# One numbering of expert blocks over eight sequences, worked off in two stages: 71 blocks a layer in place of 55 + 23

## The chip, the cores and the metric

The kernel runs on one core of a Trainium2 chip. The metric is the time of one execution on the device in microseconds (us), as a median of several runs. Profiles are taken from one further execution each. Of the core's engines, TensorE (PE) multiplies matrices and transposes, VectorE (DVE) and ScalarE (ACT) do element-wise work, GpSimd (POOL) does some of that and issues the indirect DMAs, and SyncE (SP) issues most other DMAs. PEld is TensorE's weight load, which overlaps the matmuls.

## What is computed

Input x has 8 sequences of 512 tokens with 256 features, all in float32. Four layers follow one another, each added to x:

```
x = x + attention_a(layernorm(x))   # 16 heads of 64, causal, with ALiBi
x = x + moe(layernorm(x))           # "f1"
x = x + attention_b(layernorm(x))   # 8 heads of 128, causal, rotary
x = x + moe(layernorm(x))           # "f2", the same weights

def moe(x):                         # 8 experts, each token goes to 2 of them
    h = rms_norm(x) * norm_w
    vals, idx = top_k(h @ gate_w.T + gate_b, 2)
    w = softmax(vals)
    t = h @ mlp1_w[e].T + mlp1_b[e]           # 512 wide: glu and lin
    a = min(glu, 7) * sigmoid(1.702 * glu) * (clip(lin, -7, 7) + 1)
    y[e] = a @ mlp2_w[e].T + mlp2_b[e]        # 256 wide
    return x + sum over the two experts of w * y[e]
```

The change touches the two expert layers alone. There are 8 x 512 x 2 = 8,192 pairs of a token and an expert in each.

## The kernel before, in words

**Sorted blocks.** Class `Experts` (line 533) serves one expert layer. `choose` (L645) picks each token's two experts, `count` (L701) counts how many pairs each expert has so far (`run`) and so gives each pair a place within its expert (`at`). Every expert's pairs are rounded up to whole blocks of 128 rows; a block thus has one expert and one set of weights. How many blocks each expert needs depends on the data, so the program has as many blocks as the worst case needs. The sequences form two groups, `GROUPS` (0 to 5, and 6 and 7), each numbered on its own: (6,144 + 8 x 127) / 128 gives 55 blocks, (2,048 + 8 x 127) / 128 gives 23. That is 78 blocks a layer. Each group has its own DRAM tables: `h_all` (normed rows to gather from) and `y_all` (results by token, `PLANE` rows for a token's first expert, as many for the second, and spare rows for empty slots).

**Sorting a group** (`sorting`, L865) has one piece per sequence and one more. The first piece calls `slots` (L726), which rounds the counts up, adds the expert's start to every place and splits the slot into block and row; it also gives each block's expert, by a comparison of the block's start with the experts' ends, and from it the column offsets of weights and biases (`we_at`, `be_at`). `pair` (L789) makes one-hot matrices of rows (`row`) and blocks (`col`) for one sequence, `invert` (L825) multiplies them on TensorE and adds the result into `sum`, and `tokens` (L839) turns that into the numbers of the token to gather and of the row to write. All of it but the product runs on VectorE.

**One step a block.** `run` (L984) walks n over all blocks. Step n does: `gather` of block n+4 (L886, an indirect DMA on GpSimd; 128 rows of 1 KB), `turn_act` of block n-4 (two transposes `atp` L948, ScalarE copy `aT` L952), `turn_rows` of block n (two transposes `gtp` L899, ScalarE copy back into the gather tile `g` L902), `first` of block n-1 (four matmuls recorded for `hp` L923; VectorE adds the bias L934, ScalarE's sigmoid L935, VectorE L937 to L939 make the product `a`), `second` of block n-5 (four matmuls recorded for `y` L961, VectorE adds the bias L971, GpSimd writes the rows by an indirect DMA L972), and then whatever pieces of other work are noted for step n in `aside`. Gather tiles hold `ROWS` = 4 blocks, in two buffers, and a group starts a new tile; the tiles of results `y` do the same.

**What sets the order.** TensorE's order is the program's, written out by hand (`manual_schedule` for PE). On the other engines a scheduler orders the instructions, save those that `keep_in_program_order` binds (ScalarE's copies and sigmoid among them). Each engine works in its order. `aside` places the work around the blocks: the end of the attention before (`flush`, L1125), the sort of the second group in pieces at steps 17, 21 and 25, and the start of what follows. The sort of the first group lies in the last sequences of the attention (`layer`, L1066).

**Ends of the layers.** Results may be read once all of a group's blocks are written; `read` (L1011) has a wait on every write of the group. With `done` = 55 + 6 = 61, the end of the first expert layer places in its steps: reading the rows of sequence 0 (`collect`, L1026, at done and done+1), adding them (`add`, L1042, line L1051, one 128-token tile a step from done+3), layer norm (done+8, +9, +11) and the first projections of attention b (`project` at steps 77 and 78, `values` at 80 and 81). The sequences 1 to 7 are added during attention b. At the end of f2, twelve halves of the sequences 0 to 5 are read at done + 3k/2 and finished four steps later (`finish`, L1178: four L1051 operations and an output DMA on SP, L1180); the four halves of sequences 6 and 7 are read after the last block, on SP's and ACT's queues.

## Time and profile before

| | |
|---|---|
| time, median of 3 runs | 2318.38 us (2312.13 to 2318.58) |
| time of the profiled execution | 2280.75 us |
| its span, first to last instruction | 2279.0 us |
| mean granted clock of TensorE | 0.994 |
| blocks, both layers | 156 |
| first hp of f1, last hp of f1 | at 932.7, at 1178.1 us |
| first hp of f2, last hp of f2 | at 2005.6, at 2249.4 us |
| DMA, mean over the span | 49 GB/s |

Lines of the profile name the source line of kernel.py, the engine, the operation, out <- in by the program's names, the shapes and the count; after the first bar the busy time and the mean of one in ns, after the second the engine's idle time just before, and what ended it. In a timeline the first two columns are start and duration in us. In the table of windows each engine has its busy time and count, then follow the granted clock, DMA share and GB/s. A matmul's name appears once for a run of instructions that start together ("x4"), and its duration is then that of the run. Where the profile says L923, TensorE multiplies a block by its expert's first weights; where it says L934, VectorE adds the bias to that.

### The profile page before, as it was taken

To read this page: it belongs to the slowest core of one execution; us is meant where nothing else is said; L and a number is where in the kernel's file an instruction comes from. 1 tells how busy PE (TensorE), PEld (TensorE's weight loads), DVE (VectorE), ACT (ScalarE), POOL (GpSimd) and SP (SyncE) were. 2 spreads that over 40 slices of the span, in tenths; PEclk is the share of its full clock that TensorE was granted. 3 is DMA by queue.
4 is the path that set the end of the run, shared out by engine and by line. 5 is a ranking of instruction groups with operands and counts; after the bars stand their busy time and mean duration, and the time that the engine had idled before them with its cause. 6 is when DMAs were issued, how large, how long until landed. Compare 5 with 4: busy or idle time off the path is not lost.

```text
span 2279.0 us, 34315 instructions
## 1 busy us (share of the span) xinstructions
PE 2227.7 (98%) x10681; PEld 1454.4 (64%) x10681; DVE 1597.6 (70%) x4773; ACT 972.3 (43%) x2826; POOL 995.3 (44%) x1365
## 2 busy tenths in 40 slices
PE   8999999999999999999999999999999999999995
PEld 5666666666666666666665666666666666666663
DVE  4566666666666677687777677777767678868677
ACT  4555555555555554333324334343434333433331
POOL 5443434343434342466654343333434344356663
PEclk9999999999999999999999999999999999999998
DMA  7100000000000000422320010110101000132246
GB/s 243 38 22 7 20 10 20 10 20 10 20 10 19 14 5 30 145 83 88 107 65 15 10 38 13 35 34 18 42 5 42 10 28 1 52 116 88 85 150 207
DMA packets 79731, 112.53 MB, mean 49 GB/s; under 512 B 10016, under 2 KB 64448, under 8 KB 79552
## 3 DMA queue, kind: packets, MB, share of 16 engines
q1 hardware_dynamic: 62656, 67.58, 8.9%
q0 software_dynamic: 14976, 40.91, 5.9%
q8 instruction: 89, 1.46, 0.3%
q10 hardware_dynamic: 1920, 1.84, 0.2%
q14 instruction: 90, 0.74, 0.1%
HBM read 68.86 MB, written 41.44 MB: 48 GB/s over the span
## 4 chain that ended last, share of the span: by engine, by line
PE 88%; DVE 6%; DMA 2%; issue 1%; ACT 1%; POOL 1%; SPq 0%; DVEq 0%; POOLq 0%; ACTq 0%
PE hp_f L923 10%; PE pp_b L327 9%; PE pp_a L327 9%; PE op_a L466 6%; PE tp_a L439 6%; PE sp_a L385 6%; PE sp_b L385 6%; PE op_b L466 5%; PE yp_a L484 5%; PE yp_b L484 5%; PE y_f L961 5%; PE vp_a L308 4%; PE vp_b L308 4%; PE tp_b L439 3%; PE gtp_f L899 1%; PE atp_f L948 1%
## 5 line engine op out<-in xcount | busy, mean ns | idle before, releaser
L407 ACT ACTIVATE S_a<-S_a,nm_a 128x512 f32<-128x512 f32 (+3 forms) x512 | 280.3, 549 | 311.8 <-DVE nm_a L397 311.7
L340 POOL TENSOR_TENSOR qk_b<-qk_b,rot_b 128x512 f32<-128x512 f32 x128 | 163.0, 1274 | 457.9 <-DVE qk_b L339 449.7
L923 PE MATMUL hp_f<-we,g_f 128*128 x624 | 294.7, 595 | 3.9 <-ACT g_f L902 3.9
L366 POOL TENSOR_SCALAR ali_a<-alibi 128x512 f32<-128x512 f32 x128 | 79.6, 622 | 455.6 <-DVE nm_a L397 443.1
L407 ACT ACTIVATE S_b<-S_b,nm_b 128x512 f32<-128x512 f32 (+3 forms) x256 | 142.8, 558 | 239.7 <-DVE nm_b L397 237.2
L397 DVE CUSTOM_DVE_ANT_0 S_a<-sp_a,ali_a 128x512 f32<-128x512 f32 (+3 forms) x512 | 215.8, 487 | 30.5 <-PE sp_a L385 30.5
L424 POOL TENSOR_SCALAR S_a<-S_a,sum_a 128x384 f32<-128x384 f32 x378 | 202.6, 554 | 34.9 <-DVE sum_a L418 26.4
L972 POOL DMA_INDIRECT y_f<-y_f,row_f x156 | 158.2, 1014 | 112.9 <-DVE y_f L971 67.0
L935 ACT ACTIVATE u_f<-u_f 128x256 f32<-128x256 f32 x156 | 65.1, 417 | 318.6 <-DVE u_f L934 304.8
L886 POOL DMA_INDIRECT g_f<-h_all_f,token_f x156 | 156.7, 1005 | 71.9 <-issue 68.3
L397 DVE CUSTOM_DVE_ANT_0 S_b<-sp_b,mask 128x512 f32<-128x512 f32 (+3 forms) x256 | 119.1, 484 | 90.8 <-PE sp_b L385 90.8
L385 PE MATMUL sp_b<-qk_b 128*128 128x512 f32 (+3 forms) x512 | 171.8, 438 | 8.1 <-POOL qk_b L340 8.1
L439 PE MATMUL tp_a<-ident,S_a 128*128 128x128 f32 x1280 | 166.7, 277 | 4.3 <-DVE O_a L474 3.2
L961 PEld LDWEIGHTS y_f<-we,aT_f 128*128 128x128 f32 x624 | 118.0, 190 | 82.1 <-issue 46.4
L934 DVE TENSOR_TENSOR u_f<-hp_f,be 128x512 f32<-128x512 f32 x156 | 107.8, 691 | 82.2 <-PE hp_f L923 75.1
L439 PEld LDWEIGHTS tp_a<-ident,S_a 128*128 128x128 f32 x1280 | 141.6, 141 | 35.5 <-issue 21.3
L961 PE MATMUL y_f<-we,aT_f 128*128 x624 | 160.2, 379 | 2.6 <-ACT aT_f L952 2.6
L466 PE MATMUL op_a<-PT_a,V_a 128*64 128x384 f32 (+3 forms) x1024 | 154.5, 439 | 3.6 <-ACT PT_a L449 2.2
L923 PEld LDWEIGHTS hp_f<-we,g_f 128*128 128x128 f32 x624 | 106.3, 190 | 80.7 <-issue 74.6
L385 PE MATMUL sp_a<-qk_a 64*128 64x512 f32 (+3 forms) x1024 | 155.5, 443 | 0.9 <-DVE qk_a L344 0.9
L449 ACT COPY PT_a<-tp_a 128x512 f32<-128x512 f32 (+1 forms) x320 | 139.0, 497 | 27.1 <-PE tp_a L439 26.8
L466 PE MATMUL op_b<-PT_b,V_b 128*128 128x512 f32 (+3 forms) x512 | 148.6, 433 | 0.0
(185 smaller groups left out, 4460.1 us busy)
## 6 DMA issues: line engine op xcount, KB each, us to landing
h_all_f<-hn_f SPq DMA_DIRECT2D x64, 128.0 KB, 1.7
xm_f<-x_mid_f SPq DMA_DIRECT2D x16, 512.0 KB, 4.0
yg_f<-y_f SPq DMA_DIRECT2D x32, 256.0 KB, 4.2
yg_f<-y_f SPq DMA_DIRECT2D x56, 128.0 KB, 2.2
we<-w_dram SPq DMA_DIRECT2D x8, 512.0 KB, 7.3
x_mid_f<-x SPq DMA_DIRECT2D x8, 512.0 KB, 3.4
x_mid_f<-xm_f SPq DMA_DIRECT2D x8, 512.0 KB, 2.9
x<-x_in_dram SPq DMA_DIRECT2D x7, 512.0 KB, 4.1
```

The lines of the kernel that those rows point to most:

```text
L308: nc.tensor.matmul(vp[:, k, :], lhsT=self.xT[b][:, c, t * P : (t + 1) * P], rhs=wv[:, c, q * 2 * P : (q + 1) * 2 * P], start=(c == 0), sto ...
L327: nc.tensor.matmul(pp, lhsT=w[:, c, g * P : (g + 1) * P], rhs=self.xT[b][:, c, :], start=(c == 0), stop=(c == NC - 1),)
L340: nc.gpsimd.tensor_tensor(qk[:, j, :], qk[:, j, :], rot, ALU.add)
L385: nc.tensor.matmul(sp[i][:, at[it] : at[it] + w], lhsT=qk[r, 0, it * P : (it + 1) * P], rhs=qk[r, 1, 0:w], start=True, stop=True,)
L397: nc.vector.tensor_tensor_reduce(out=s, in0=sp[i][:, at[it] : at[it] + w], in1=add[i][:, T - w : T], scale=scale, scalar=float(np.finfo(np ...
L407: nc.scalar.activation(s, s, AF.Exp, bias=nm[:, it : it + 1], scale=-1.0, accum_out=sums[:, it : it + 1],)
L424: eng.tensor_scalar(s, s, sums[:, it : it + 1], 1.0, ALU.mult, ALU.mult)
L439: nc.tensor.transpose(tp[:, o : o + P], S[:, S_OFF[it] + jt * P : S_OFF[it] + (jt + 1) * P], ident,)
L466: nc.tensor.matmul(op[i * cols : (i + 1) * cols, jt * P : T], lhsT=v[:, jt, c0 : c0 + cols], rhs=PT[i][:, P_OFF[jt] : P_OFF[jt] + T - jt * P],
L484: nc.tensor.matmul(yp[:, 0:D], lhsT=o[:, c, t * P : (t + 1) * P], rhs=wo[:, half * HALF + c, :], start=(c == 0), stop=(c == HALF - 1),)
L923: nc.tensor.matmul(hp, lhsT=h[:, c * P : (c + 1) * P], rhs=we_sb[:, bass.DynSlice(wat + c * 2 * FI, 2 * FI)], start=(c == 0), stop=(c == N ...
L961: nc.tensor.matmul(yp, lhsT=aT[:, c * P : (c + 1) * P], rhs=we_sb[:, bass.DynSlice(wat + NC * 2 * FI + c * D, D)], start=(c == 0), stop=(c ...
```

## The change

The eight sequences now have one numbering of blocks a layer, (8,192 + 8 x 127) / 128 = 71, which is worked off in two stages. The numbers go first to the blocks that the first six sequences fill entirely (of each expert in turn), then to each expert's one begun block, then to blocks that only the last two sequences need. Of the first six sequences' 6,144 pairs at most 8 x 127 are in begun blocks, so at least 41 blocks (`FULL`) are always full: stage 0 is blocks 0 to 40, stage 1 is the 30 others, whose rows may come from all eight sequences. The pairs of the first six lie in the first 55 blocks (`TOUCHED`), so their one-hot matrices stay 55 wide; those of the last two are 30 wide (`REACH`). There is one `h_all` and one `y_all` a layer.

A new piece `sizes` rounds the counts down and up, keeps three sizes for each expert and the running ends and shifts over the 3 x 8 of them, and calls `experts`, which in stage 1 compares each block with 24 ends. `slots` makes three products and reductions for each of a token's two choices, where there was one. Stage 0's sort has one piece more, in the attention; stage 1's has four, at steps 16, 20, 24 and 28. `done` is 60. Reads of the first six sequences wait for the first 55 writes and are declared independent of the later ones. The end of f1 is closer together (add at 63 and 64, norm at 65, 66 and 68, `project` at 69 and 70, `values` at 73 and 74). The last step is 75; of f2's twelve halves eight are finished at steps 64 to 74, and four after the last step. Line numbers move: L886 becomes L936, L899 L949, L902 L952, L923 L973, L934 to L939 become L984 to L989, L948 and L952 become L998 and L1002, L961 L1011, L971 and L972 become L1021 and L1022, L1013 L1067, L1051 L1107, L1180 L1233.

The core of the diff; what is cut renames the tables, opens them once for all sequences and passes `sum` by slices.

```diff
-GROUPS = [(0, 6), (6, 8)]
-BLOCKS = [(2 * (hi - lo) * T + NE * (P - 1)) // P for lo, hi in GROUPS]
-NJ = max(BLOCKS)
-PLANE = 32 * P
+STAGES = [(0, 6), (6, NB)]
+PAIRS = 2 * STAGES[0][1] * T
+SPARE = NE * (P - 1)
+FULL = -((SPARE - PAIRS) // P)
+TOUCHED = (PAIRS + SPARE) // P
+TOTAL = (2 * NB * T + SPARE) // P
+BLOCKS = [FULL, TOTAL - FULL]
+FIRST = [0, FULL]
+REACH = [(0, TOUCHED), (FULL, TOTAL)]
+PLANE = NB * T
...
-            self.h_all = [
-                dram.tile([(hi - lo) * T, D], F32, tag=f"h_{kind}_{i}", name=f"h_all_{kind}_{i}")
-                for i, (lo, hi) in enumerate(GROUPS)
-            ]
-            self.y_all = [
-                dram.tile([2 * PLANE + n * P, D], F32, tag=f"y_{kind}_{i}", name=f"y_{kind}_{i}")
-                for i, n in enumerate(BLOCKS)
-            ]
-            self.group_of = {b: i for i, (lo, hi) in enumerate(GROUPS) for b in range(lo, hi)}
...
+        def blocks_up(self, i, out, counts, add):
+            whole = self.rt(i, [P, NE], "whole", I32)
+            nc.vector.tensor_scalar_add(whole, counts, float(add))
+            nc.vector.tensor_scalar(
+                whole, whole, 7, 7, ALU.logical_shift_right, ALU.logical_shift_left
+            )
+            nc.vector.tensor_copy(out, whole)
+        def sizes(self, i):
+            r = self.R
+            size, end, shift, up = r["size"], r["end"], r["shift"], r["up"]
+            limit = self.rt(i, [P, NE], "limit")
+            turn = self.rt(i, [P, NE], "turn")
+            if i == 0:
+                nc.vector.memset(r["sum"], 0.0)
+                nc.vector.memset(size[:, 2, :], 0.0)
+                self.blocks_up(i, size[:, 0, :], r["run"], 0)
+                self.blocks_up(i, up, r["run"], P - 1)
+                nc.vector.tensor_tensor(size[:, 1, :], up, size[:, 0, :], ALU.subtract)
+                nc.vector.tensor_copy(limit, size[:, 0, :])
+            else:
+                self.blocks_up(i, size[:, 2, :], r["run"], P - 1)
+                nc.vector.tensor_tensor(size[:, 2, :], size[:, 2, :], up, ALU.subtract)
+                nc.vector.tensor_copy(limit, up)
+            flat = [x.rearrange("p a e -> p (a e)") for x in (end, size, shift)]
+            nc.vector.tensor_tensor_scan(
+                flat[0], ones[:, 0 : 3 * NE], flat[1], 0.0, ALU.mult, ALU.add
+            )
+            nc.vector.tensor_tensor(flat[2], flat[0], flat[1], ALU.subtract)
+            nc.vector.tensor_tensor(shift[:, 1, :], shift[:, 1, :], size[:, 0, :], ALU.subtract)
+            nc.vector.tensor_tensor(shift[:, 2, :], shift[:, 2, :], up, ALU.subtract)
+            nc.vector.tensor_tensor(turn, shift[:, i + 1, :], shift[:, i, :], ALU.subtract)
+            self.moves = shift[:, i, :], limit, turn
+            self.experts(i)
+        def experts(self, i):
...
+            parts = 1 if i == 0 else 3
+            ends = r["end"].rearrange("p a e -> p (a e)")[:, 0 : parts * NE]
             expert = self.rt(i, [P, nj], "expert")
-            for j0 in range(0, nj, 32):
-                j1 = min(j0 + 32, nj)
-                wide = [P, j1 - j0, NE]
+            most = D // (parts * NE)
+            for j0 in range(0, nj, most):
+                j1 = min(j0 + most, nj)
+                wide = [P, j1 - j0, parts * NE]
                 past = work.tile(wide, F32, tag="kb", bufs=8, name=f"past_{kind}_{i}_{j0}")
                 nc.vector.tensor_tensor(
                     past,
-                    end.unsqueeze(1).to_broadcast(wide),
-                    step_p[:, j0:j1].unsqueeze(2).to_broadcast(wide),
+                    ends.unsqueeze(1).to_broadcast(wide),
+                    step_p[:, FIRST[i] + j0 : FIRST[i] + j1].unsqueeze(2).to_broadcast(wide),
...
+            if parts > 1:
+                number = self.rt(i, [P, nj], "number", I32)
+                nc.vector.tensor_copy(number, expert)
+                nc.vector.tensor_single_scalar(number, number, NE - 1, ALU.bitwise_and)
+                nc.vector.tensor_copy(expert, number)
...
+        def slots(self, i):
+            kind = self.kind
+            r = self.R
+            lo, hi = STAGES[i]
+            here = slice(lo * NT, hi * NT)
+            n = (hi - lo) * NT
+            for k in range(2):
+                own = work.tile([P, 3, n], F32, tag="kb", bufs=8, name=f"own_{kind}_{i}_{k}")
+                for m, move in enumerate(self.moves):
+                    o = work.tile([P, n, NE], F32, tag="kb", bufs=8, name=f"of_{kind}_{i}_{k}_{m}")
+                    nc.vector.tensor_tensor(
+                        o, r["pick"][k][:, here, :], move.unsqueeze(1).to_broadcast([P, n, NE]), ALU.mult
+                    )
+                    nc.vector.tensor_reduce(own[:, m, :], o, AX.X, ALU.add)
+                by, limit, turn = (own[:, m, :] for m in range(3))
+                at = r["at"][:, k, here]
+                nc.vector.tensor_tensor(limit, at, limit, ALU.is_ge)
+                nc.vector.tensor_tensor(turn, turn, limit, ALU.mult)
+                nc.vector.tensor_tensor(by, by, turn, ALU.add)
+                nc.vector.tensor_tensor(at, at, by, ALU.add)
+            number = work.tile([P, 2, 2, n], I32, tag="kb", bufs=8, name=f"number_{kind}_{i}")
+            low, high = number[:, 0], number[:, 1]
+            nc.vector.tensor_copy(high, r["at"][:, :, here])
+            nc.vector.tensor_single_scalar(low, high, P - 1, ALU.bitwise_and)
+            nc.vector.tensor_single_scalar(high, high, 7, ALU.logical_shift_right)
+            nc.vector.tensor_copy(r["low"][:, :, here], low)
+            nc.vector.tensor_copy(r["high"][:, :, here], high)
...
-            here = slice(s * NT, (s + 1) * NT)
+            r, here = self.place(s)
+            j0, j1 = REACH[i]
+            nj = j1 - j0
...
         def sorting(self, i):
-            n = GROUPS[i][1] - GROUPS[i][0]
+            lo, hi = STAGES[i]
             def piece(s):
-                if s == 0:
+                if s == lo:
                     self.slots(i)
-                if s < n:
+                if s < hi:
                     self.pair(i, s)
-                if s > 0:
+                if s > lo:
                     self.invert(i, s - 1)
-                if s == n:
+                if s == hi:
                     self.tokens(i)
-            return [lambda s=s: piece(s) for s in range(n + 1)]
+            return [lambda: self.sizes(i)] + [lambda s=s: piece(s) for s in range(lo, hi + 1)]
...
-                in_=self.h_all[i],
-                in_offset=bass.IndirectOffsetOnAxis(ap=self.R[i]["token"][:, j : j + 1], axis=0),
+                in_=self.h_all[0 : STAGES[i][1] * T, :],
+                in_offset=bass.IndirectOffsetOnAxis(ap=self.R["token"][i][:, j : j + 1], axis=0),
...
+            if len(self.writes) >= TOUCHED:
+                tc.declare_no_dep(
+                    made.ins, group=f"reads_{self.kind}", reason="no rows of the first stage"
+                )
+            self.writes.append(made.ins)
...
+            early = b < STAGES[0][1]
+            writes = self.writes[0 : TOUCHED if early else TOTAL]
+            for write in writes:
...
+            if early:
+                for write in self.writes[TOUCHED:]:
+                    tc.declare_no_dep(made.ins, write, reason="no rows of the first stage")
+                tc.add_to_no_dep_group(f"reads_{self.kind}", made.ins)
...
-        at = [(6, 7, 1), (7, 0, 1), (7, 1, 1), (7, 2, 1), (7, 3, 1), (7, 4, 1), (7, 6, 1)]
+        at = [(6, 7, 1), (6, 7, 2), (7, 0, 1), (7, 1, 1), (7, 2, 1), (7, 3, 1), (7, 4, 1), (7, 6, 1)]
...
-            aside[17 + 4 * n] = [piece]
+            aside[16 + 4 * n] = [piece]
...
-    done = BLOCKS[0] + 6
+    done = TOUCHED + 5
...
     aside[done] = [lambda: exp_a.fetch(0)]
     for k, tag in enumerate(("xT", "PT")):
         tt = (2 * k, 2 * k + 1)
-        aside.setdefault(done + k, []).append(
-            lambda tt=tt, tag=tag: exp_a.collect(0, tt, tag, both_queues)
-        )
-        for t in tt:
-            aside.setdefault(done + t + 3, []).append(lambda tt=tt, t=t: exp_a.add(0, tt, (t,)))
-    aside[done + 8] = [lambda: att_b.norm(0)]
-    aside[done + 9] = [lambda: att_b.apply(0)]
-    aside[done + 11] = [lambda: att_b.turn_norm(0)]
+        aside[done].append(lambda tt=tt, tag=tag: exp_a.collect(0, tt, tag, both_queues))
+        aside[done + 3 + k] = [lambda tt=tt: exp_a.add(0, tt)]
+    aside[done + 5] = [lambda: att_b.norm(0)]
+    aside[done + 6] = [lambda: att_b.apply(0)]
+    aside[done + 8] = [lambda: att_b.turn_norm(0)]
     for k in range(2):
-        aside[sum(BLOCKS) - 1 + k] = [lambda k=k: att_b.project(0, 0, k)]
-        aside[sum(BLOCKS) + 2 + k] = [lambda k=k: att_b.values(0, 0, k)]
+        aside[TOTAL - 2 + k] = [lambda k=k: att_b.project(0, 0, k)]
+        aside[TOTAL + 2 + k] = [lambda k=k: att_b.values(0, 0, k)]
     exp_a.run(aside)
...
-    end = sum(BLOCKS) + 5
+    end = TOTAL + 5
     exp_b.run(aside)
     for m in range(end, n + 5):
         for piece in aside.get(m, ()):
             piece()
-    last = [(b, tt) for b in range(*GROUPS[1]) for tt in ((0, 1), (2, 3))]
+    last = [(b, tt) for b in range(*STAGES[1]) for tt in ((0, 1), (2, 3))]
```

## The prediction

> **What bounds the kernel now.** I read the page first: engine shares, the chain that ended last, then the expert rows.
>
> ```profile
> PE 2227.7 (98%) x10681; PEld 1454.4 (64%) x10681; DVE 1597.6 (70%) x4773; ACT 972.3 (43%) x2826; POOL 995.3 (44%) x1365
> ...
> PE 88%; DVE 6%; DMA 2%; issue 1%; ACT 1%; POOL 1%; SPq 0%; DVEq 0%; POOLq 0%; ACTq 0%
> ...
> L923 PE MATMUL hp_f<-we,g_f 128*128 x624 | 294.7, 595 | 3.9 <-ACT g_f L902 3.9
> ```
>
> TensorE is busy 98% and holds 88% of the chain; 624 first-layer matmuls are 4 for each of 156 blocks (2 x 78). All idle time ahead of them is 3.9 us. So a block less is time less, unless something now hidden comes out. The table of windows for 90 us of undisturbed blocks, then their timeline, give the price of one and the room beside it:
>
> ```profile
> 1020.00:1110.00 90.00, 90.00 (x359) 56.79 (x359) 63.58 (x153) 28.55 (x90) 58.71 (x60) 1.00 0.28 87
> ```
>
> ```profile
> 1084.09 1.88 PE L923 MATMUL hp_f<-we,g_f 128*128 x4
> ...
> 1086.01 0.69 DVE L934 TENSOR_TENSOR u_f<-hp_f,be 128x512 f32<-128x512 f32 x1 [0.81 <-PE hp_f L923]
> ...
> 1086.74 0.98 POOL L886 DMA_INDIRECT g_f<-h_all_f,token_f  x1 [1.16 <-issue]
> 1086.79 0.42 ACT L935 ACTIVATE u_f<-u_f 128x256 f32<-128x256 f32 x1 [2.07 <-DVE u_f L934]
> ...
> 1087.11 1.88 PE L923 MATMUL hp_f<-we,g_f 128*128 x4
> 1087.12 0.35 ACT L952 COPY aT_f<-atp_f 128x256 f32<-128x256 f32 x1
> ...
> 1087.37 0.38 ACT L902 COPY g_f<-gtp_f 128x256 f32<-128x256 f32 x1
> ...
> 1089.03 0.69 DVE L934 TENSOR_TENSOR u_f<-hp_f,be 128x512 f32<-128x512 f32 x1 [0.77 <-PE hp_f L923]
> ```
>
> TensorE is full (90.00 of 90). A block takes 1087.11 - 1084.09 = 3.02 us, in both layers. VectorE has 0.69+0.29+0.42+0.42+0.42 = 2.24 us in a step, so 0.78 to spare. ScalarE works in order: its copy L902 stands behind the sigmoid L935, which waits for L934. By the timeline the hp after next starts no earlier than 1.8 us after L934 starts; L934 starts 1.92 after its own hp. VectorE may thus lag by 2 x 3.02 - 1.8 - 1.92 = 2.3 us before TensorE stops. GpSimd has about 2.6 us of 3.02 (0.98 + 0.99 and 0.30 before each).
>
> [...] 8 elements take 0.16 us, 256 take 0.42; the new sort is made of such operations. [...] Trace: a gather lands a median 2.8 us after issue, a scattered write 2.4. [...] Trace: after TensorE's 3.39 us wait at 1200.19 a pair of score matmuls took 2.07 us instead of 1.02.
>
> **The change, part by part** (against the profiled execution: span 2279.0, its time 2280.75; the median 2318.38 is 1.0165 of that).
>
> 1. *Seven blocks a layer fewer.* The built order has 154 fewer TensorE rows, 14 blocks of 11. 14 x 3.02 = **-42.3**. Their gathers, writes, VectorE and ScalarE work lay beside TensorE and give nothing more.
>
> 2. *Sort of stage 1 (sizes, slots, pairs, tokens), beside the blocks.* Before, by the VectorE rows: slots 4.7 us, pairs 4 x (0.72 + 3 x 0.25) = 5.9, the two additions 0.4, tokens 9 x 0.18 = 1.6: 12.6. After: sizes 1.9 of small ones, comparisons of 240 elements 3 x 0.8 = 2.4, number 0.6, where 0.7, together 5.6; slots 2 x (3 x 0.43 + 4 x 0.16) + 0.9 = 4.8; pairs 30 wide 6.1; rest 2.1: 18.6. What matters is the crowding: in the built order sizes and slots, 10.4 us, stand in seven steps (after the L934 of blocks 13 to 19). These spare 7 x 0.78 = 5.5; 4.9 is left, less the lag that is allowed. L934 of block 13 already lags 2.44 instead of 1.92, so 1.8 is left: TensorE stops 3.1. The same sum for before (5.5 extra in four steps, 3.1 spare, 1.8 allowed) gives 0.6, and the trace has 0.54 at block 18 of the first layer (0.16 in the second), so I trust it. The later pieces (steps 24, 28) come as the lag is used up by then and drained: nothing. Per layer 3.1 - 0.5: **+5.3** for both, bounds +2 (operations overlap more) and +8.
>
> 3. *Stage boundary at 41.* Rows are gathered into tiles of four blocks, two buffers, and a stage starts a new tile. 41 leaves a tile with one block (55 left three). Block 41's tile takes the buffer of blocks 36 to 39, free at the end of block 39's hp in step 40; its own transpose stands in step 41, behind second (0.86) and a transpose (0.22), 1.1 us later. Trace: from an hp's end (1085.97) to the gather that it frees 0.77, landing 2.75: 3.5. TensorE waits 3.5 - 1.1 = 2.4 a layer, **+4.8**. On GpSimd the write of block 35 queues behind that gather; its readers are far off. Bounds: 0 (the gather issued at once and landing early) and 5.4 a layer (the longest landing, 5.7). The tile of results has the same shape of ring: block 41's addition needs block 39's write landed, 6.0 us apart, against some 3.3 to issue and 2.5 to land. VectorE may wait there, inside its 2.3 us: nothing, bound +2 a layer.
>
> 4. *Both numberings merged: sort of stage 0 in attention.* Three products and reductions per choice instead of one, 192 elements at 0.35: 2 x 2 x 0.70 = 2.8, small ones about 2.5: some 5 us more VectorE a layer, over seven pieces. In the first attention TensorE waited for next to nothing there, in the second 2.6 us: **+1**, bounds 0 and +2. Fewer tables, one memset less: nothing, VectorE hides them.
>
> 5. *End of the first layer.* From done to turn_norm are 8 steps, not 11; additions in two steps instead of four. 8 x 0.48 + 4 x 0.61 + 4 x 0.40 = 7.9 us of VectorE in steps 63 to 66 with 3.1 spare: 4.8 lag, over 2.3 allowed: TensorE stops 2.5, where the steps around turn_norm before lost 1.0: **+1.6**, bounds 0 and +4. The two reads of 256 KB now go on SP's queue together, 0.5 us apart; nothing waits behind them. ScalarE's V copy, 4.94 us on a write at 1189, and TensorE's 0.86 behind it, go as values come four steps after project with fewer writes ahead: **-0.9**, bounds -0.9 and 0.
>
> 6. *End of the second layer.* Of twelve finishes eight stand in the steps and four after the last; all twelve stood inside. VectorE is less crowded, so the last addition of y comes 2.5 us earlier than the blocks alone give (before, steps 70 to 76 lost 2.6). But the tail shows who waits:
>
> ```profile
> 2260.93 0.41 DVE L971 TENSOR_TENSOR y_f<-y_f,be 128x256 f32<-128x256 f32 x1
> ...
> 2262.16 0.97 POOL L972 DMA_INDIRECT y_f<-y_f,row_f  x1 [0.30 <-issue]
> 2264.75 1.91 SPq L1013 DMA_DIRECT2D yg_f<-y_f  x4
> ...
> 2267.77 0.48 DVE L1051 SCALAR_TENSOR_TENSOR xm_f<-yg_f,wt_f,xm_f 128x256 f32<-128x256 f32 x1 [6.03 <-DMA yg_f<-y_f]
> ```
>
> Four finishes (16 x 0.47 = 7.5) fill the 6.03 us in which VectorE idles. But their output DMAs stand on SP's in-order queue between the last reads, and each waits for its additions: I get 20.5 us from the last addition to the end instead of 17.7: +2.9. Net **+0.4**, bounds -2.5 and +4.
>
> Sum: -42.3 + 5.3 + 4.8 + 1.0 + 1.6 - 0.9 + 0.4 = -30.1. Scaled by 1.0165: -30.6, so 2318.4 - 30.6 = **2288**.
>
> **The rivals.**
> - *A, the sum*: 2288 (2281 to 2294).
> - *B, the cover holds.* VectorE is busy 64 of 90 us and ScalarE 29, and the 2.3 us of lag swallow the rest; the boundary gather is early. Only the blocks count: -42.3 x 1.0165 = -43.0: 2275 (2270 to 2281). Against it: ScalarE's order, which already cost 0.54 with a smaller sort.
> - *C, the boundary is worse.* The gather lands after 5.7 us: TensorE waits 5.4, and its clock halves[...]. That is 7.1 - 2.4 = 4.7 more a layer: -20.7, 2297 (2294 to 2304). For it: GpSimd has 0.4 us a step free, and the longest landing is in the trace. Against it: the median is 2.8.
> - *D, slower: the early reads wait for all 71 writes*, since one table now holds both stages. First layer: 6.5 us from last addition to read issue (as at 1120.19 to 1126.73), then 15 us of read, addition, norm with TensorE idle: 21.5. Second: 24 reads and 12 outputs, 9.4 MB at the 207 GB/s of the page's last slice, 45 us behind the end. +66 - 30 = +36: 2355. It decides once over half of that waits. Against it: the dependences name the first 55 writes, and by-table waits worked before (the read left 2.9 us after block 54's write was issued).
> - That the change doesn't remove what it says is excluded by the 154 rows.
>
> **The numbers.** A 0.50, B 0.24, C 0.22, D 0.02, rest 0.02. Predicted 2288. A, B and C give 2270 to 2303 with little left out. A measurement here tells about 0.3% (7 us) from no change: faster 0.96, same 0.02, slower 0.02.
>
> **What would show it.** The starts of hp block by block: 3.02 us, stops of some 3 us between blocks 15 and 21, named as waiting for ScalarE's g copy; one of 2.4 at block 41, transpose waiting for a gather; some 2.5 near step 68. From the last addition of y to the end: 20.5 us. No stop at 41 or under 1 us of stops by block 21 would prove the steps wrong; reads that are issued after the last write would prove D.

## The result, and the profile after

| | time before, measured beside it | time after | ratio |
|---|---|---|---|
| result | 2315.33 us | 2296.6 us | 0.9918 [0.9898, 0.9938] |
| repeated (e5) | 2316.02 | 2295.0 | 0.9915 [0.9894, 0.9935] |
| repeated (e10) | 2314.91 | 2292.79 | 0.9900 [0.9884, 0.9915] |

The change saves some 20 us, two thirds of what was forecast. The kernel before takes about 2280 us at some times and about 2315 at others, on one and the same chip (e1 and e5), so a time is compared only with times of before that were taken beside it, and a trace only with one of the same kind.

The page of the kernel after: its first row, its chain and its row of first-layer matmuls.

```profile
PE 2206.9 (96%) x10513; PEld 1436.2 (63%) x10513; DVE 1581.7 (69%) x4797; ACT 962.2 (42%) x2784; POOL 961.0 (42%) x1337
...
PE 85%; DVE 8%; DMA 2%; issue 2%; ACT 2%; another core or an unknown queue 1%; POOL 1%; SPq 0%; DVEq 0%; ACTq 0%; POOLq 0%
...
L973 PE MATMUL hp_f<-we,g_f 128*128 x568 | 277.4, 612 | 28.3 <-ACT g_f L952 22.1
```

568 first-layer matmuls instead of 624: 14 blocks less, as forecast. But most of the 28.3 us of idle time in that row, against 3.9 in the row of before that the prediction showed, is not the change's. The profile of before that the prediction stood on took 2280.75 us, where the median was 2318.38; the profile of after took 2297.31 us, as long as its other runs. A trace of before that took 2316.85 us (e11) has 24.8 us of idle time in the same row, so setting the first two profiles side by side would have blamed the change for some 20 us that it never cost.

The fair comparison cuts the span at events that both kernels have: the starts of the first and last `hp` of each expert layer and the gate matmuls `lp_f` of sequence 0 in the second attention, all from the timeline. Two pairs, each measured together: before and the one-ring variant (e1, e2; before at 2280 us), before and after (e11, e10; before at 2315), in us. After itself has no trace beside a before of 2280 us; there e2, which is after without its stop at block 41, stands in for it.

| stretch | e1 before | e2 | difference | e11 before | e10 after | difference |
|---|---|---|---|---|---|---|
| to the first hp | 933.4 | 932.0 | -1.4 | 935.2 | 934.2 | -1.0 |
| first layer, first to last hp | 245.3 | 226.0 | -19.3 | 261.9 | 245.6 | -16.3 |
| last hp to gates of sequence 0 | 166.2 | 162.4 | -3.8 | 166.4 | 162.4 | -4.1 |
| those gates to the second layer's first hp | 661.2 | 670.2 | **+9.0** | 661.1 | 670.3 | **+9.2** |
| second layer, first to last hp | 243.2 | 221.3 | -21.9 | 260.6 | 246.0 | -14.6 |
| last hp to the end | 30.4 | 35.7 | **+5.4** | 29.9 | 35.6 | **+5.8** |
| span | 2279.7 | 2247.6 | -32.1 | 2315.1 | 2294.1 | -21.0 |

Seven blocks at 3.02 us are 21.1 a layer. So the layers gave less than that in after, the second attention took 9 back and the tail 5 to 6. The waits behind these numbers stand below, with the experiments on them.

Two rows need care. The first row's 1.0 to 1.4 us is no gain of the change: in the first pair it is there already at the first gates of the first layer (185.6 us in e2, 187.0 in e1), before any sorting, and three traces of before differ by as much (186.2, 187.0, 187.3). And 1.2 us or so of the third row is TensorE's clock, which was halved there for 6.83 us in before and for 3.41 in e2 and e10 (last section).

The tail of after, by its timeline: the same kinds of lines as those shown of before.

```profile
2271.60 0.41 DVE L1021 TENSOR_TENSOR y_f<-y_f,be 128x256 f32<-128x256 f32 x1
...
2272.30 0.96 POOL L1022 DMA_INDIRECT y_f<-y_f,row_f  x1 [0.95 <-DVE y_f L1021]
...
2278.16 5.78 ACTq L1067 DMA_DIRECT2D yg_f<-y_f  x4
...
2282.90 0.90 SPq L1067 DMA_DIRECT2D yg_f<-y_f  x2
...
2288.30 3.75 DVE L1107 SCALAR_TENSOR_TENSOR xm_f<-yg_f,wt_f,xm_f 128x256 f32<-128x256 f32 x8 [1.40 <-DMA yg_f<-y_f]
```

Before, the reads of the last rows began 2.6 us after the last write (2262.16 to 2264.75) and were out within 2 us. Now the first goes 5.9 us after it (2272.30 to 2278.16) and the last pair on SP 10.6 us after it.

### The profile page after: what moved, and what is told of

It reads as the page before. It is cut to its first block, busy times and chain, and to the rows that moved or that the text cites. A ratio compares the mean times of both kernels' runs of the same rounds, so it can differ in the third digit from the quotient of the medians.

```text
span 2295.5 us, 33708 instructions
## 1 busy us (share of the span) xinstructions
PE 2206.9 (96%) x10513; PEld 1436.2 (63%) x10513; DVE 1581.7 (69%) x4797; ACT 962.2 (42%) x2784; POOL 961.0 (42%) x1337
## 3 DMA queue, kind: packets, MB, share of 16 engines
q10 hardware_dynamic: 1920, 1.84, 0.2%
## 4 chain that ended last, share of the span: by engine, by line
PE 85%; DVE 8%; DMA 2%; issue 2%; ACT 2%; another core or an unknown queue 1%; POOL 1%; SPq 0%; DVEq 0%; ACTq 0%; POOLq 0%
PE hp_f L973 9%; PE pp_b L335 9%; PE pp_a L335 9%; PE op_a L474 6%; PE tp_a L447 6%; PE sp_b L393 6%; PE sp_a L393 6%; PE op_b L474 5%; PE yp_b L492 5%; PE yp_a L492 5%; PE vp_a L316 4%; PE vp_b L316 4%; PE y_f L1011 4%; PE tp_b L447 3%; PE gtp_f L949 2%
## 5 line engine op out<-in xcount | busy, mean ns | idle before, releaser
L973 PE MATMUL hp_f<-we,g_f 128*128 x568 | 277.4, 612 | 28.3 <-ACT g_f L952 22.1
L1022 POOL DMA_INDIRECT y_f<-y_f,row_f x142 | 142.3, 1002 | 156.3 <-DVE y_f L1021 97.0
L985 ACT ACTIVATE u_f<-u_f 128x256 f32<-128x256 f32 x142 | 59.2, 417 | 271.1 <-DVE u_f L984 213.0
L447 PE MATMUL tp_a<-ident,S_a 128*128 128x128 f32 x1280 | 166.4, 277 | 4.8 <-DVE O_a L482 3.2
L984 DVE TENSOR_TENSOR u_f<-hp_f,be 128x512 f32<-128x512 f32 x142 | 98.0, 690 | 104.5 <-PE hp_f L973 43.2
L936 POOL DMA_INDIRECT g_f<-h_all_f,token_f x142 | 141.1, 994 | 62.7 <-issue 55.8
L973 PEld LDWEIGHTS hp_f<-we,g_f 128*128 128x128 f32 x568 | 98.5, 194 | 105.8 <-issue 75.5
L1011 PEld LDWEIGHTS y_f<-we,aT_f 128*128 128x128 f32 x568 | 110.1, 195 | 76.5 <-issue 51.7
L1011 PE MATMUL y_f<-we,aT_f 128*128 x568 | 149.4, 387 | 1.8 <-ACT aT_f L1002 1.8
```

The source lines that it names most:

```text
L447: nc.tensor.transpose(tp[:, o : o + P], S[:, S_OFF[it] + jt * P : S_OFF[it] + (jt + 1) * P], ident,)
L973: nc.tensor.matmul(hp, lhsT=h[:, c * P : (c + 1) * P], rhs=we_sb[:, bass.DynSlice(wat + c * 2 * FI, 2 * FI)], start=(c == 0), stop=(c == N ...
L1011: nc.tensor.matmul(yp, lhsT=aT[:, c * P : (c + 1) * P], rhs=we_sb[:, bass.DynSlice(wat + NC * 2 * FI + c * D, D)], start=(c == 0), stop=(c ...
```

## Experiments

In the kernels of the experiments line numbers lie a few lines further than in after (L973 is L974 in e3, L1067 is L1080 in e9).

**Before against itself (e1_before_again).** No edit: it shows how small a difference can be told.

> The kernel before, unchanged. Its one profiled execution had a span of 2279.0 us and 2280.75 us of time, its other runs 2312 to 2318 us; the kernel after was profiled at 2297.3 us, as long as its other runs, and shows stops in which VectorE and ScalarE get TensorE's results 2 to 4 us late although TensorE's records go on every 3.02 us. Theory S (such stops are part of the usual execution of both kernels, and the profiled execution of before was free of them by luck): the profile here has a span of about 2311 us and 30 us or more of stops among the expert blocks, at the same places of the block sequence as after (blocks 9 and 15 to 18), so that the change took 15 to 20 us from like executions. Rival T (they come from the change): the expert blocks of before are as even as in its first profile (under 1 us of stops between blocks 13 and 66 of the first layer) and the 35 us lie in the attention layers or ahead of them.

Measured: 2279.39 us against 2279.74, ratio 0.9998 [0.9989, 1.0006]. Its trace gives the left half of the table.

**One numbering for the buffers too (e2_one_ring).** Only the boundary at block 41 is undone: tiles of gathered rows and of results are counted over both stages, so that no tile is begun with one block in it.

```diff
-            if j % ROWS == 0:
-                self.rows[i, j // ROWS] = work.tile(
+            q = FIRST[i] + j
+            if q % ROWS == 0:
+                self.rows[q // ROWS] = work.tile(
...
-                self.ys[i] = work.tile([P, ROWS, D], F32, tag="V", name=f"y_{key}")
-            y = self.ys[i][:, j % ROWS, :]
+                self.ys[0] = work.tile([P, ROWS, D], F32, tag="V", name=f"y_{key}")
+            y = self.ys[0][:, q % ROWS, :]
```

> After, with the gather tiles and the tiles of results numbered over both stages, so that block 40 shares its tiles with blocks 41 to 43. After stopped at the boundary for 3.15 + 1.74 us in the first layer and 3.15 + 1.45 in the second (gaps between the starts of hp 39, 40 and 41 above 3.02). My theory (the gather of block 41 comes late because its tile takes a buffer that comes free in step 40): both stops go, 9.5 us less than after, some 2287 us. Rival (the gather is late for another reason, its token numbers or GpSimd's queue): the stop stays, 0 to 2 us less. Second rival (the engines only shift the stop to the next block): 0.

Measured: 2251.41 us against 2279.74, 0.9874 [0.9858, 0.9891]. From block 38 to 42 every hp starts 3.01 or 3.02 us after the one before it, in both layers: the stop is gone. The interval lies below two of after's three and overlaps the third a little (0.9891 against 0.9884); e3, which keeps the boundary (and moves other work) and was measured beside it, took 7.7 us more. What stays of the change's costs in this run, 9.0 and 5.4 us, belongs to other parts. The windows of 90 us of its undisturbed blocks are as full as those of before:

```profile
1010.00:1100.00 90.00, 90.00 (x375) 57.18 (x373) 67.28 (x174) 29.40 (x93) 59.74 (x59) 1.00 0.27 87
```

**The experts of stage 1 later (e3_experts_late)**, boundary kept: the comparisons that give each block its expert leave the crowded steps.

```diff
-            self.experts(i)
+            if i == 0:
+                self.experts(i)
...
             aside[16 + 4 * n] = [piece]
+        aside[32] = [lambda: exp.experts(1)]
```

> After, with the comparison of the blocks with the 24 ends (experts of stage 1, some 3.7 us of VectorE) moved from step 16 to step 32, after the sort. After stops for 1.05 + 0.60 + 0.90 + 0.25 = 2.8 us between hp 15 and hp 19. My theory (sizes and slots crowd VectorE in steps 14 to 20): 3.7 us less stands there, those stops fall to 0.5 us or less a layer, nothing new at step 32, 4 to 5 us less than after in both layers, some 2292 us. Rival (the stops belong to count and choose, which stand at steps 11 to 14): they stay, no change.

Measured: 2259.12 us against 2279.74, 0.9908 [0.9892, 0.9925]: the same ratio as after's. Blocks 13 to 21 lose 2.4 and 2.0 us beyond 3.02, not less than in e2 (1.6 and 1.2). The room was taken by the slots: their products and reductions stand in the steps of blocks 15 to 17 in this trace, in e2 in those of 16 to 18. So this remedy did not test what it was meant to; e8 comes closer.

The run has the boundary beside a before of 2280 us. Its timeline at block 41 of the first layer (start, duration, engine, line, operation, idle before and who ended it):

```profile
1065.73 0.99 POOL L937 DMA_INDIRECT g_f<-h_all_f,token_f  x1 [1.16 <-PE hp_f L974]
...
1068.56 0.44 PE L950 MATMUL gtp_f<-ident,g_f 128*128 128x128 f32 x2 [2.52 <-DMA g_f<-h_all_f,token_f]
...
1069.17 2.69 PE L974 MATMUL hp_f<-we,g_f 128*128 x4 [0.17 <-issue]
...
1071.65 1.91 PE L1012 MATMUL y_f<-we,aT_f 128*128 x4
...
1073.95 1.88 PE L974 MATMUL hp_f<-we,g_f 128*128 x4
```

and its windows there (length, then busy time of PE, PEld, DVE, ACT, POOL; granted clock, DMA share, GB/s):

```profile
1066.00:1070.00 4.00, 1.30 (x5) 0.69 (x5) 1.14 (x4) 0.83 (x3) 3.08 (x4) 1.00 0.23 66
1070.00:1074.00 4.00, 4.00 (x12) 2.41 (x11) 1.39 (x4) 0.48 (x2) 2.67 (x4) 0.57 0.32 98
```

The same block in the second layer, by timeline and window:

```profile
2129.72 0.44 PE L950 MATMUL gtp_f<-ident,g_f 128*128 128x128 f32 x2 [2.49 <-DMA g_f<-h_all_f,token_f]
...
2130.32 1.96 PE L974 MATMUL hp_f<-we,g_f 128*128 x4 [0.17 <-issue]
...
2131.00:2135.00 4.00, 3.77 (x14) 2.15 (x14) 2.28 (x5) 1.00 (x3) 2.88 (x3) 1.00 0.33 100
```

Here is the forecast wait, in mechanism and size: the gather is released by the end of an hp, issued, and TensorE stands 2.52 us at the transpose of its rows (forecast 2.4). The forecast lacked two things. In the first layer the clock is 0.57 over the 4 us after the stop: the hp takes 2.69 instead of 1.88 us and the y 1.91 instead of 1.03. In the second layer the clock stays at 1.00 after a stop of the same length, and the boundary still costs more than its wait: from the start of the transposes to that of the hp it takes 0.60 us (2129.72 to 2130.32) where 0.22 is usual, and at the next block TensorE waits 0.23 us for ScalarE's copy aT. The two steps over the boundary last 6.09 + 4.78 us in the first layer and 6.06 + 3.48 in the second, that is 4.8 and 3.5 more than two blocks. In the three traces of after they cost 4.9 and 4.6 (its first profile), 3.2 and 3.7 (e5), 4.4 and 4.9 us (e10).

**Both (e4_ring_late).** The edits of e2 and e3 together.

> Both edits of the two runs above. My theory: their gains add, 9.5 + 4.5 = 14 us less than after, some 2283 us. Rival (one of them only uncovers the other or a stop behind it): the sum is at least 4 us short of the two alone.

Measured: 2253.35 us against 2279.74, 0.9881 [0.9865, 0.9898], 1.9 us above e2 with overlapping intervals. Blocks 13 to 21 lose 2.4 and 2.0 us as in e3, so nothing is gained over e2. Against e3, from which it differs by the boundary alone, it takes 5.8 us less. The two traces differ by more than that within the expert layers, 8.3 us; e4 lost 3.2 of it again after the first layer, where its clock was halved for 6.83 us and e3's was not at all.

**After again (e5_after_again).** No edit.

> The kernel after, unchanged, on a chip where before may run at 2280 us as in its first profile (the last call's chip) instead of 2315. There the one-ring kernel took 2251.4 us; its trace lacks the two stops at the boundary of the stages, 4.9 + 4.6 us. Theory S (on the first chip results came late in both kernels, by about as much): after is 20 us faster than before here as well, 2260 us where before takes 2280, and has no stops of over 1 us at blocks 9, 15, 22, 25, 47, 51 of the first layer, but keeps the stops at 39 and 40. Rival (the late results hit after alone, and before by chance): it takes 2297 us or is 30 us faster.

Measured: 2295.0 us against 2316.02, 0.9915 [0.9894, 0.9935]. Before took 2316 us beside it, so what was to be seen, after beside a before of 2280 us, stays unmeasured.

**The sort of stage 0 one piece later (e6_ring_sort0)**, on top of e2: five products of the sort stand one place later, and the first of them no longer at the head of sequence 7. The numbering itself (`sizes`, `slots`) stays where it was.

```diff
-        at = [(6, 7, 1), (6, 7, 2), (7, 0, 1), (7, 1, 1), (7, 2, 1), (7, 3, 1), (7, 4, 1), (7, 6, 1)]
+        at = [(6, 7, 1), (6, 7, 2), (7, 1, 1), (7, 2, 1), (7, 3, 1), (7, 4, 1), (7, 5, 1), (7, 6, 1)]
```

> The one-ring kernel with the products of stage 0's sort (invert) in the last sequence of each attention one or two groups later, so that VectorE has more time between a sequence's one-hot matrices and TensorE's use of them. In the one-ring kernel TensorE waits 4.9 + 1.7 us for col at the first product in attention b, and the step from the gates of sequence 6 to those of sequence 7 is 115.7 us where before needs 106.7. My theory (sizes and three-fold slots stand ahead of that product, the wait is all of it): 6 to 9 us less than one-ring, 2243 to 2246 where before takes 2280. Rival (VectorE is behind over the whole sequence, the wait moves to a later product or to the scores): less than 2 us.

Measured: 2277.11 us against 2316.02, 0.9832 [0.9812, 0.9851]. The view of the tile `inv_f`, the sort's product on TensorE, says what it was. In after:

```profile
L879 PE MATMUL inv_f<-col_f,row_f x128: 189/211/298, 819.2 to 2110.6; 128*128 128x110 bf16 x96, 128*128 128x60 bf16 x32
its engine sat idle before it (us, times) until:
  DVE col_f L864: 6.9, 2
```

In e6, and in before, no name stands under "sat idle before it". The gates of sequences 5 and 6 in the second attention, between which this product lies, are 107.6 us apart in e6, 115.9 in after (e10) and 106.7 in before (e11): 8.4 of the 9.2 us are this one stop. (Up to the second layer's first hp e6 is 7.7 us shorter than e10.) Where it comes from is in e10's timeline, from the start of the numbering to the product:

```profile
1888.21 0.17 DVE L736 TENSOR_SCALAR whole_f<-run_f 128x8 int32<-128x8 f32 x1
...
1912.17 1.15 DVE L864 TENSOR_TENSOR col_f<-col_f,tiles 128x220 bf16<-128x220 bf16 x1
...
1913.38 0.50 PE L879 MATMUL inv_f<-col_f,row_f 128*128 128x110 bf16 x4 [4.97 <-DVE col_f L864]
```

and in before (e11) from the same start to the same product:

```profile
1909.64 0.17 DVE L734 TENSOR_SCALAR count_f<-run_f 128x8 int32<-128x8 f32 x1
...
1923.68 0.58 DVE L816 TENSOR_TENSOR col_f<-col_f,tiles 128x220 bf16<-128x220 bf16 x1
...
1929.88 0.56 PE L830 MATMUL inv_f<-col_f,row_f 128*128 128x110 bf16 x8
```

In both kernels TensorE comes to the product 20.2 us after the numbering starts (in e10 at 1908.41, where its 4.97 us of waiting begin). In before the first operand is ready after 14.6 us, so 5.6 us were free; in after it is ready after 25.1. The chain is 10.5 us longer, about twice the 5 us of VectorE's work that the prediction counted. It has almost no gap on VectorE, and the attention's own operations stand between its links, as the end of e10's chain shows (qk_b is the attention's):

```profile
1907.03 0.93 DVE number_f L828
...
1910.24 0.59 DVE row_f L847
...
1911.13 0.60 DVE qk_b L347
...
1912.26 1.06 DVE col_f L864
```

The next product waits another 1.74 us. The rest of the 9.2 is the clock: the windows of e10 show 0.50 from 1914 to 1920, where TensorE did 4.4 us of work at half pace, some 2.2 us.

**The last reads ahead of the outputs (e7_ring_tail)**, on top of e2: the four `collect` of sequences 6 and 7 are issued before the pieces that remain after the last step.

```diff
-    for m in range(end, n + 5):
-        for piece in aside.get(m, ()):
-            piece()
     last = [(b, tt) for b in range(*STAGES[1]) for tt in ((0, 1), (2, 3))]
     for b, tt in last:
         exp_b.collect(b, tt, "S", (nc.sync, nc.scalar))
+    for m in range(end, n + 5):
+        for piece in aside.get(m, ()):
+            piece()
```

> The one-ring kernel with the last reads (sequences 6 and 7) put ahead of the four finishes that follow the last step, in the program's order. In one-ring the end comes 23.5 us after the last addition of y, in before 17.7. My theory (SyncE's queue holds reads of the last sequences behind output DMAs that wait for additions): the tail falls to 18 to 19 us, 4.5 to 5.5 us less than one-ring, 2246.5 where before takes 2280. Rival (the reads wait for the last write, not for the queue; the tail is VectorE's 16 + 16 additions and transfers): less than 1.5 us.

Measured: 2292.14 us against 2316.02, 0.9902 [0.9882, 0.9922]: 15.0 us more than e6 beside it, of which some 8 are e6's edit, that e7 lacks. From the start of the last y addition to the end it takes 28.0 us, where after has 23.9 and before 18.0 to 18.8 in its three traces (the prediction's 17.7 counts from the end of that addition). Its timeline:

```profile
2271.83 0.46 SPq L1070 DMA_DIRECT2D yg_f<-y_f  x1
...
2277.34 8.73 DVE L1110 SCALAR_TENSOR_TENSOR xm_f<-yg_f,wt_f,xm_f 128x256 f32<-128x256 f32 x19 [7.82 <-DMA yg_f<-y_f]
```

The last addition of the early sequences still stands ahead on VectorE, and its read now goes last. VectorE idles 7.82 us for it, then has 19 additions in a row.

**Stage-1 sort spread out and held in place (e8_ring_spread)**, on top of e2: sizes, slots (in two parts), pairs, tokens and experts at seven steps. Bound to program order are the first instruction of sizes, the products of slots, the comparisons of experts, and with them VectorE's bias addition of every block (L984 in after).

```diff
+                if i == 1:
+                    tc.keep_in_program_order(made)
...
+            made = nc.vector.tensor_tensor(t, hp, be_sb[:, bass.DynSlice(bat, 2 * FI)], ALU.add)
+            tc.keep_in_program_order(made)
...
-        for n, piece in enumerate(exp.sorting(1)):
-            aside[16 + 4 * n] = [piece]
+        first, *rest = exp.sorting(1)
+        late = [lambda: exp.slots(1, (0,)), lambda: exp.slots(1, (1,)), *rest, lambda: exp.experts(1)]
+        for n, piece in zip((15, 17, 19, 21, 25, 29, 32), (first, *late), strict=True):
+            aside[n] = [piece]
```

> The one-ring kernel with stage 1's sort spread: the additions L934 (u) and the first operation of each part are bound to the program's order, sizes at step 15, the halves of slots at 17 and 19, pairs at 21 and 25, tokens at 29, the comparison with 24 ends at 32. Between two u additions stand at most 2.5 us of sort, never two heavy ones in a row. The one-ring kernel stops for 0.40 + 0.90 + 0.24 us at blocks 16 to 18 of the first layer, 0.89 + 0.25 in the second. My theory (the crowding of VectorE makes these stops): they fall under 0.3 us a layer, 2 us less in all, 2249.5. Rival (the stops come from ScalarE or TensorE's own inserts): they stay.

Measured: 2279.31 us against 2316.02, 0.9848 [0.9829, 0.9866]. Excess over 3.02 us of the steps after blocks 15 to 20, first layer:

```
before (e11)   0.96  0.33  0.32  0.75  0.10  0.25
after  (e10)   1.22  0.58  0.91  0.24  0.10  0.00
e6             1.06  0.59  0.92  0.23  0.10  0.00
e8             0.00  0.31  0.10  0.65  0.10  0.19
```

Spread out, the stops fall from 2.9 us (e6) to 1.35, and in the second layer from 2.8 to nothing, where under 0.3 a layer was expected; in e9 and e12, which hold the same edit, 1.4 and 1.8 us stay. So the order on VectorE makes them, though the binding of the bias additions, which is in the same edit, isn't told apart from the spreading. The rows also warn: before has 2.7 us there itself (2.3 in the second layer), so beside it the change adds only 0.3 and 0.5; between e1 and e2 it adds 0.8 a layer. The first layer as a whole is 6.9 us shorter than in e6 (237.7 against 244.6), more than this. Most of the rest is in the stops at blocks 25 and 26 (4.7 us in e6, 0.1 in e8), of the kind that the last section describes; one trace of each doesn't show whether the edit removed these. In time e8 isn't told apart from e2 (0.9874 [0.9858, 0.9891]).

**Three edits and outputs on another queue (e9_all_four)**: e2, e6 and e8 together, and the outputs of the four late finishes issued by GpSimd instead of SP.

```diff
-        aside.setdefault(n + 4, []).append(lambda b=b, tt=tt: finish(b, tt, nc.sync))
+        engine = nc.sync if n + 4 < TOTAL + 5 else nc.gpsimd
+        aside.setdefault(n + 4, []).append(lambda b=b, tt=tt, engine=engine: finish(b, tt, engine))
```

> The one-ring kernel with the later products of stage 0's sort, the spread sort of stage 1, and the output DMAs of the four finishes after the last step on GpSimd's queue instead of SyncE's. The first three edits were measured alone; the last is new. From its trace: before ends 17.7 us after the last addition of y, after 22.3 to 23.5, and putting the last reads first made it 28.0. My theory (the reads of the last sequences wait in SyncE's in-order queue behind output DMAs that wait for additions): without these in the queue the tail is 18 to 19.5 us. In all: 2238 to 2242 us where before takes 2280, 2264 to 2270 where it takes 2316. Rival for the tail (the four reads of ScalarE's queue and the transfers set it, or GpSimd's output DMAs are slow): 22 us or more, 2243 to 2247 or 2268 to 2274.

Measured: 2272.87 us against 2314.91, 0.9823 [0.9809, 0.9837]; 19.9 us under after beside it. But the tail, counted as above, is 23.1 us: little came of moving the outputs. The reads stand alone on SP and still take 11.70 us to be issued, by its timeline, and its waits say for what: the last write, and an earlier read that has to land first.

```profile
2247.03 11.70 SPq L1080 DMA_DIRECT2D yg_f<-y_f  x7
...
SPq L1080 <- DMA yg_f<-y_f: 4.5, 1, 4.5
SPq L1080 <- DMA y_f<-y_f,row_f: 3.2, 1, 3.2
```

**Both kernels beside each other (e10_after_third, e11_before_third).** No edit; the traces of the right half of the table.

> The kernel after once more, to have a trace of it from executions in which before takes 2280 us, if these are such. Theory S (as for the earlier run of it): 2258 to 2261 us beside 2280, stops at blocks 15 to 18 and 39 to 40 only, 6.6 us of waiting for col in attention b, a tail of 23 us. If before takes 2316 us here: 2295 as twice before.

> The kernel before once more, to have a trace of it from executions in which it takes 2316 us, if these are such. Theory S: some 35 us of stops, most of them among the 156 expert blocks with results of TensorE that arrive 1 to 4 us late, at blocks 9, 15 to 18 and then every four blocks or so, as after has them. Rival T: even blocks, and the time lies in the attention layers. If before takes 2280 us here: as its first profile.

Measured: 2292.79 us against 2314.91, 0.9900 [0.9884, 0.9915]; before, in a single execution, 2316.85. The row of first-layer matmuls of before in e1 (2281.46 us):

```profile
L923 PE MATMUL hp_f<-we,g_f 128*128 x624 | 294.7, 595 | 3.2 <-ACT g_f L902 3.1
```

and in e11:

```profile
L923 PE MATMUL hp_f<-we,g_f 128*128 x624 | 300.0, 603 | 24.8 <-ACT g_f L902 18.8 <-issue 4.6 <-ACT aT_f L952 1.1
```

The kernel is the same. So of the 22.1 us behind ScalarE's copy in the profile of after some 19 say nothing of the change.

**Additions on GpSimd (e12_pool_adds)**: e2, e6 and e8, and the last two early finishes (eight additions and their outputs) computed and issued by GpSimd.

```diff
+                    if by is nc.gpsimd:
+                        g, w = got[:, k, n, :], self.R["w"][k][:, m : m + 1]
+                        by.tensor_scalar(g, g, w, 1.0, ALU.mult, ALU.mult)
+                        by.tensor_tensor(xs, g, xs, ALU.add)
+                        continue
```

> The one-ring kernel with the later products of stage 0's sort and the spread sort of stage 1, and the additions of sequence 5 (the last two of the four finishes after the last step) on GpSimd, with their output DMAs on its queue: 16 of its operations of about 0.36 and 0.72 us in place of 8 of VectorE of 0.47. Two changes of the order in the queues did not shorten the tail (28.0 and 23.1 us, where after has 22 to 23.5 and before 17.7). My theory now (the tail is VectorE's: 33 additions are left after the last addition of y, 17 in before, and the late halves' reads land in between, so VectorE idles twice): the additions of sequences 6 and 7 start as soon as their reads land, and the tail is 19.5 to 20.5 us; 0.981 of before. Rival (the reads of sequences 6 and 7 land late because 13 transfers crowd the queues): 22 us or more, 0.983 or the 0.982 of the kernel with the outputs on GpSimd's queue.

Measured: 2272.08 us against 2315.56, 0.9809 [0.9795, 0.9822], the lowest ratio of all here: 1.9% under before, with twice after's gain. The tail is not what gave it: 24.4 us. VectorE, now relieved, idles 7.17 us for a read before its last 16 additions. It isn't told apart from e9 (0.9823 [0.9809, 0.9837]).

## Why the prediction was right or wrong

The direction and its reason were right; the gain was forecast at 30 us and is 20. The measured 2296.6 us lies outside the range given for the sum A (2281 to 2294) and within C's; that 2270 to 2303 together held it is due to C's share, and C's own sum is not what happened. Term by term, in us, from the pair e1 and e2 (boundary from the traces that have it):

| step of the prediction | forecast | measured |
|---|---|---|
| 1. fourteen blocks | -42.3 | -42.3 (14 x 3.02) |
| 2. sort of stage 1 | +5.3 | +2.1 |
| 3. boundary at 41 | +4.8 | +8.3 (e3), +9.4 (e10), +6.9 (e5) |
| 4. sort of stage 0 | +1.0 | **+9.0** |
| 5. end of the first layer | +0.7 | -3.1 |
| 6. end of the second layer | +0.4 | +3.6 |
| start, not forecast | 0 | -1.4 to -1.0 |
| sum | -30.1 | -23.8 (e3) to -22.3 (e10); spans e10 less e11 -21.0 |

The rows are cuts of one span, so that they add up proves nothing. They show where the forecast was off: steps 3, 4 and 6 cost some 15 us more than forecast, and steps 2 and 5 some 7 us less. That these errors ran against each other is luck.

*1. Right.* 56 hp matmuls less, and 3.02 us a step in after too, wherever nothing stops it.

*2. Right mechanism, too large.* The stops lie where they were forecast and name ScalarE's g copy, and in e8 another order on VectorE makes them shrink. From block 15 to 28 the two layers lose 3.9 us in e2 against 1.8 in before (e1), so +2.1. That is the lower bound, whose reason was that operations overlap more than their sum says. They do overlap by a little (in the trace of before L971 starts at 1086.98, 0.08 us before L937 ends), but that this made the difference was the author's estimate and isn't shown. The later pieces cost nothing, as forecast: the 0.25 us at blocks 23 and 27 is TensorE's own work for the sort, without a wait, and before has the same 0.24 at blocks 20 and 24. That after's traces show the forecast 3 us of stops between blocks 15 and 21 (3.05 and 2.8 in e10) is no confirmation, as before has 2.7 and 2.3 there beside it.

*3. Right mechanism, too small.* The wait was 2.5 to 2.6 us for 2.4 forecast. But here a stop cost more than its wait. Where the clock stayed full (e3's second layer, both layers of e5) the boundary cost 3.2 to 3.7 us a layer, where it was halved 4.4 to 4.9. The clock was left out of the sum and put into rival C, behind a wait of 5.4 us, as 1.7 of its 7.1 us, which no trace had shown by then. It was halved at five of the eight boundary stops of these traces, after waits of 2.5 to 2.6 us; at the first of after's first profile for 3.4 us, that is 1.7 us of work. The extra wait of the y tile didn't show: in e3's first layer the addition of block 41 starts 0.03 us after the operation ahead of it. e2, which joins both tiles, leaves nothing at these blocks. (The prediction gives 2.4 us as a scattered write's median landing; by that trace it is 2.5, which moves no term.)

*4. The step that failed.* "In the first attention TensorE waited for next to nothing there, in the second 2.6 us: +1, bounds 0 and +2." Work was counted (5 us of VectorE), spread over seven pieces and called hidden. But TensorE, which works in its order, meets the sort's first product at the head of sequence 7, and that product needs the whole chain of numbering. In the second attention 5.6 us were free there, and the chain became 10.5 us longer. All of the excess comes out at one place, 6.7 us of waiting and some 2 of clock. In the first attention the chain grew as much (first operand 56.2 us after the gates of sequence 5 in e10, 45.9 in e11), but TensorE comes to the product only at 61.4, and nothing is lost. e6 confirms the place: with the products one place later 8.4 us return.

*5. Right to name the V copy; the stop that was forecast did not come.* TensorE's 0.86 at 1190.08 is gone, as forecast. But the 2.5 us of TensorE's waiting near step 68 are not there: in e2 TensorE has no gap from 1134 us, six blocks and more ahead, to the last hp at 1158.0.

```profile
1134.00:1158.00 24.00, 24.00 (x96) 14.97 (x95) 22.72 (x59) 6.72 (x20) 12.70 (x14) 1.00 0.20 56
```

VectorE was as crowded as forecast (6.00 of the first 6 us), but what it was late with stopped nothing. Before waits 0.56 us at block 68; that went too, with some 0.4 us of its aftermath. The remaining 1.2 us are the clock again: after the 3.3 us wait for GpSimd, which is still there, it was halved for 6.83 us in before (both pairs) and for 3.41 us in e2 and e10. Together -3.1.

*6. Half right.* Steps 70 to 76 of before lost 2.0 to 2.6; that went (-1.8). The tail was forecast to grow by 2.9 and grew by 5.4. The reason given, outputs that wait for their additions between the last reads on SP, is there: in e10 SP's last reads go 6.1 to 10.8 us after the last write, and without the outputs (e9) three of the four are out after 6.9. But the tail stays at 23.1 us, at 24.4 when additions leave VectorE as well (e12), and 28 when the reads are put first (e7). What the traces show instead is a crowd of transfers. The windows of e10 at its end:

```profile
2270.00:2276.00 6.00, 0.00 (x0) 0.00 (x0) 4.80 (x12) 0.00 (x0) 1.97 (x2) 0.66 1.00 340
2276.00:2282.00 6.00, 0.00 (x0) 0.00 (x0) 3.57 (x8) 0.00 (x0) 0.00 (x0) 0.50 0.85 275
2282.00:2288.00 6.00, 0.00 (x0) 0.00 (x0) 4.28 (x11) 0.00 (x0) 0.00 (x0) 0.50 1.05 353
```

and those of before (e11) in the same phase:

```profile
2297.00:2303.00 6.00, 0.00 (x0) 0.00 (x0) 0.52 (x2) 0.00 (x0) 1.61 (x2) 0.50 0.59 180
2303.00:2309.00 6.00, 0.00 (x0) 0.00 (x0) 4.65 (x11) 0.00 (x0) 0.00 (x0) 0.50 1.04 342
```

Before, the early finishes were over and one burst remained, at 342 GB/s. After, the 16 DMA engines are nearly full from the last write on (shares of 0.85 to 1.05), and the last reads seem to join a line. It begins with the last write itself, for which all these reads wait: it landed 2.4 us after its issue in before (its first profile), 4.7 in e2 and 5.4 in e3, where the first reads follow 0.3 us later. By e10's view of SP's waits:

```profile
SPq L1067 <- DMA y_f<-y_f,row_f: 2.1, 1, 2.1
```

Four finishes at the end thus seem to cost not their additions but their bytes: with their outputs issued by GpSimd instead of SP (e9) the tail was 23.1 us, against 23.9 in after. One of e9's last reads also waited 4.5 us for an earlier read to land. Whether such waits or the full engines alone set the tail stays open.

*Rivals.* B (the cover holds) fell by the stops at 15 to 20 and at 41. C was right that the clock counts and wrong on the landing: in e3 TensorE went on 2.83 us after the issue of block 41's gather (1065.73 to 1068.56), where before's median landing is 2.8; its time, 2297, is the measured one, but by another sum, whose largest missing part, 8 of some 10 us, is step 4's. D was excluded: reads are issued before the last writes in every trace.

## What to carry to other kernels

When work is added beside a full engine, the sum of the added time tells little. Find the first instruction on the full engine that consumes the result, follow its whole chain backwards in the trace, and compare two times: when the chain is done, and when the full engine comes to that instruction. Here 5.6 us were free and the chain grew by 10.5; moving the products one place later was worth 8 us, against 2 for all the crowding elsewhere. Price a stop of TensorE with its restart and its clock, not only with its wait (here 3.2 to 4.9 us for a wait of 2.5 to 2.6). And before blaming a change for idle time in a row, look for the same row in a second trace of the kernel before.
